# Column quarters for the variances and attn3's row sums, and 1 / sigma through DRAM

## The chip, the cores and the metric

The kernel runs on one core of a Trainium2 chip. A core has five engines that run their own streams of instructions in order and wait for each other on semaphores: TensorE (PE, matmuls; PEld is its weight loads), VectorE (DVE), ScalarE (ACT), GpSimd (POOL) and SyncE (SP, which here issues nearly all DMAs). SBUF holds the working data in 128 partitions, PSUM takes the results of matmuls in banks of 128 x 512 f32, DRAM is the memory off the core. The metric is the device time of one execution in microseconds (us), as a median over runs.

## The reference

Two layers over x, a tensor of 2 images x 512 channels x 2048 positions (tokens) in f32. Layer 0 is softmax attention of 8 heads with 64 channels each. Layer 1 is Nystrom attention with 256 landmarks and a feed-forward step. Each of layer 1's two steps starts with a layer normalization over the 512 channels of a token:

```python
def _ln_t(v, eps=1e-5):
    m = jnp.mean(v, axis=-1, keepdims=True)
    s = jnp.var(v, axis=-1, keepdims=True)
    return (v - m) / jnp.sqrt(s + eps)
...
qL = q.reshape(b, h, m, l, d).sum(axis=3) / l
kL = k.reshape(b, h, m, l, d).sum(axis=3) / l
attn1 = softmax(einsum('bhid,bhjd->bhij', q, kL), axis=-1)
attn2 = softmax(einsum('bhid,bhjd->bhij', qL, kL), axis=-1)
attn3 = softmax(einsum('bhid,bhjd->bhij', qL, k), axis=-1)
attn2_pinv = moore_penrose_iter_pinv(attn2, PINV_ITERS)
out = attn1 @ (attn2_pinv @ (attn3 @ v))
...
t = t + _L1_attn_ref(_ln_t(t), L1_attn_Wqkv, L1_attn_Wout, L1_attn_bout, L1_attn_conv_w)
t = t + _L1_ffn_ref(_ln_t(t), L1_ffn_qidx, L1_ffn_scales, L1_ffn_W)
```

The pseudo-inverse is six iterations of products of 256 x 256 matrices. A convolution of v over 33 tokens is added to layer 1's attention.

## The kernel before

Channels lie in the partitions, tokens along the free dimension. A token block is 512 tokens (TB); an image has four of them. Heads are taken in pairs of 2 x 64 channels, four pairs an image. Everything is f32. The order of instructions on PE, DVE, ACT and POOL is the order in which the program writes them; generators that yield are interleaved by hand to fill one stage's waits with another's work. SP's DMAs are put in order by a scheduler that goes by when they can start. A DMA that waits on SP holds back the ones behind it.

The stages that matter here, in order of time:

- Attention of layer 0 (attention0, up to 1400 us): groups of two steps of scores (L1057), exp on ACT (L1065), a running sum on DVE (L1075) and values (L1087). At the end of a token block the sums over the keys are taken with line 778 (sums_of), inverted (L1102) and spread over the partitions with eight DMAs (L789, spread).
- First normalization, layer 0's output projection with it (norm0_steps over statistics; L956 is the projection yp, L963 adds the residual). For image 0 it is interleaved with attention (787 to 960 us), for image 1 with the projections of layer 1's first pairs (1405 to 1530 us). It calls statistics once a block: adds of channels on DVE (L974, L975), a matmul with a matrix of 1/512 that gives the mean on all partitions (L978), subtraction (L979), squares on ACT (L982, L985), adds (L987, L988), a second matmul for the variance (L991), sqrt on ACT (L993). The reciprocal (L1008) follows one step later, then the products on POOL (L1010) and DVE (L1011) and the store of xh. The squares lie in the buffer of x itself, xb; for image 0 there is one such buffer, and the next block's x is loaded into it (L1021) as soon as the squares are read.
- Layer 1's pairs (1740 to 2600 us): for each of eight pairs the iterations of the inverse (pinv, L1513 to L1536, tiles M and R, product banks pa and pb). Between its steps chunk(c) and last(i) put the next pair's attn3 (L1352, L1366, L1373), the previous pair's attn1 (L1580 to L1617, with sums_of and spread once a block), a convolution (L1450) and the values of the pair after next (L941). At chunk(4) landmarks_values takes attn3's row sums (L1397), inverts them (L1407) and multiplies (L1408, yT); at last(1) it transposes yT (L1416) and loads A for the next pair, which iteration_start turns into M (L1487).
- Finish: output projection of layer 1 (L956), statistics again (the squares are in an own tile sq, the reciprocal is L1641), feed-forward matmuls on the normalized but not yet divided tokens (L1673) and then the product with 1 / sigma (L1662, y), the residual add (L1663) and the store. For image 1 the four blocks lie between the last pairs, for image 0 they are the end of the kernel (from 2660 us). 1 / sigma is thus needed on all 128 partitions for each of 512 tokens.

The matmul with 128 columns of equal weights writes the same sums into all 128 partitions. sums_of instead uses 32 columns per part of the tokens, with the parts beside each other in the array; each part's sums then lie in 32 partitions alone, which is why a spread follows.

Of the kernel before, what the change touches and what calls it, by code (L numbers as in the profile page):

```python
# [10 lines left out]
F32 = mybir.dt.float32  # L11
I32 = mybir.dt.int32
AF = mybir.ActivationFunctionType
ALU = mybir.AluOpType
AX = mybir.AxisListType

P = 128
# [3 lines left out]
HEADS, D = 8, 64  # L21
NPAIR = HEADS // 2
TB = 512
NTB = S // TB
NST = S // P
LM, POOL = 256, S // 256
# [627 lines left out]
Q = P // 4  # L654
# [9 lines left out]
def fast_path(  # L664
# [35 lines left out]
    nc = tc.nc  # L700
    dram = ctx.enter_context(tc.tile_pool(name="dram1", bufs=1, space=bass.MemoryType.DRAM))
# [25 lines left out]
    def chunked(ap):  # L727
        return ap.rearrange("(k p) n -> p k n", p=P)

    def bank(name):  # L730
        return ps.tile([P, 512], F32, tag="pp", name=name)
# [17 lines left out]
    def exps(name):  # L749
        p = ppool.tile([P, 4 * (LM + 1)], F32, tag="p", name=name)  # L750
        return p[:, :1024].rearrange("p (h n) -> p h n", h=2)
# [4 lines left out]
    def row_of(name):  # L756
        return apool.tile([P, TB], F32, tag="rinv", name=name, bufs=3)

    mean_w = const.tile([P, P], F32, name="mean_w1")
    nc.vector.memset(mean_w, 1.0 / C)  # L760
    ones = const.tile([P, D], F32, name="ones1")
    nc.vector.memset(ones, 1.0)
    eps = const.tile([P, 1], F32, name="eps1")
# [5 lines left out]
    csum = const.tile([P, B * NPAIR, 4], F32, name="csum1")  # L769


    def sums_of(rs, acc):


        for h in range(2):
            for j in range(2):
                lo = h * D + j * Q
                nc.tensor.matmul(  # L778
                    rs[lo : lo + Q, :LM], lhsT=ones[:, :Q], rhs=acc[:, h, j * LM : (j + 1) * LM],
                    start=True, stop=True,  # L780
                )

    def spread(dst, few):

        for h in range(2):
            for to in range(2):
                for j in range(2):
                    lo, src = h * D + to * Q, h * D + j * Q
                    nc.sync.dma_start(dst[lo : lo + Q, j * LM : (j + 1) * LM], few[src : src + Q, :])  # L789


    def advance(gens, n=1):
# [13 lines left out]
    def drain(gen):  # L806
        for _ in gen:
            pass
# [159 lines left out]
    def deviation(name):  # L968
        return apool.tile([P, TB], F32, tag="rstd", name=f"rstd_{name}", bufs=1)

    def statistics(xb, xn, part, name, squares, row):


        nc.vector.tensor_tensor(part, xb[:, :2, :], xb[:, 2:, :], ALU.add)  # L974
        nc.vector.tensor_tensor(part[:, 0, :], part[:, 0, :], part[:, 1, :], ALU.add)  # L975
        yield
        mean = bank(f"mean_{name}")
        nc.tensor.matmul(mean, lhsT=mean_w, rhs=part[:, 0, :], start=True, stop=True)  # L978
        nc.vector.tensor_tensor(xn, xb, mean.unsqueeze(1).to_broadcast([P, KC, TB]), ALU.subtract)  # L979
        yield  # L980
        sq, *others = squares()
        nc.scalar.activation(sq, xn[:, :2, :], AF.Square)  # L982
        n = 2 // len(others)
        for i, other in enumerate(others):
            nc.scalar.activation(other, xn[:, 2 + i * n : 2 + (i + 1) * n, :], AF.Square)  # L985
            to = sq[:, i * n : (i + 1) * n, :]
            nc.vector.tensor_tensor(to, to, other, ALU.add)  # L987
        nc.vector.tensor_tensor(sq[:, 0, :], sq[:, 0, :], sq[:, 1, :], ALU.add)  # L988
        yield
        var = bank(f"var_{name}")  # L990
        nc.tensor.matmul(var, lhsT=mean_w, rhs=sq[:, 0, :], start=True, stop=True)  # L991
        rstd = row()
        nc.scalar.activation(rstd, var, AF.Sqrt, bias=eps, scale=1.0)  # L993
        yield rstd

    def out0_units(b, t, xb, oTs):
# [4 lines left out]
    def norm0_steps(b, t, xb, xn, part):  # L1001

        toks = slice(t * TB, (t + 1) * TB)
        name = f"n0_{b}_{t}"
        squares = lambda: (xb[:, :2, :], xb[:, 2:, :])
        for rstd in statistics(xb, xn, part, name, squares, lambda: deviation(name)):
            yield
        nc.vector.reciprocal(rstd, rstd)  # L1008
        wide = rstd.unsqueeze(1).to_broadcast([P, 2, TB])
        nc.gpsimd.tensor_tensor(xn[:, 2:, :], xn[:, 2:, :], wide, ALU.mult)  # L1010
        nc.vector.tensor_tensor(xn[:, :2, :], xn[:, :2, :], wide, ALU.mult)  # L1011
        nc.gpsimd.dma_start(chunked(xh_d[b])[:, :, toks], xn)
        yield
# [185 lines left out]
    class Pair:  # L1199
# [192 lines left out]
        def landmarks_values(self):  # L1392

            rs = bank(f"rs3_{self.name}")
            for j in range(2):
                for h in range(2):
                    nc.tensor.matmul(  # L1397
                        rs[h * D : (h + 1) * D, :LM],
                        lhsT=ones,
                        rhs=self.acc3[:, h, j * LM : (j + 1) * LM],  # L1400
                        start=j == 0,
                        stop=j == 1,
                    )
            rinv = self.acc3[:, 0, :]
            yT = rinv[:, LM:]
            nc.scalar.copy(rinv[:, :LM], rs[:, :LM])
            nc.vector.reciprocal(rinv[:, :LM], rinv[:, :LM])  # L1407
            nc.vector.tensor_tensor(yT, self.av3[:, :LM], rinv[:, :LM], ALU.mult)  # L1408
            X = exps(f"X2_{self.name}").rearrange("p a b -> p (a b)").rearrange("p (h k n) -> p h k n", h=2, k=2)
            self.X = [X[:, h] for h in range(2)]  # L1410
            for h in range(2):
                nc.sync.dma_start(self.X[h], X_d[self.b, self.hp, h])
            yield
            tp = bank(f"tp_{self.name}")
            for t in range(2):
                nc.tensor.transpose(tp[:, t * P : (t + 1) * P], yT[:, t * P : (t + 1) * P], ident)  # L1416
            self.Y = lmpool.tile([P, 2, P], F32, tag="Y", name=f"Y_{self.name}")
            nc.scalar.copy(self.Y, tp[:, :LM].rearrange("p (t n) -> p t n", t=2))
            A = zpool.tile([P, 2, 2, LM + 1], F32, tag="Q", name=f"A_{self.name}")
            self.A = [A[:, h] for h in range(2)]  # L1420
            for h in range(2):
                for t in range(2):
                    cols = slice(t * P, LM)
                    nc.sync.dma_start(self.A[h][:, t, cols], A_d[self.b, self.hp, h][:, t, cols])
            yield
# [193 lines left out]
    class Finish1:  # L1619
# [13 lines left out]
        def steps(self, row):  # L1633
            def squares():
                sq = apool.tile([P, 2, TB], F32, tag="acc", name=f"sq_{self.name}")
                return sq, *(row_of(f"sq{k}_{self.name}").unsqueeze(1) for k in (2, 3))

            self.xn = self.xn()
            for rstd in statistics(self.xb, self.xn, self.xn[:, :2, :], self.name, squares, row):
                if rstd is not None:  # L1640
                    nc.vector.reciprocal(rstd, rstd)  # L1641
                    self.rstd = rstd
                yield

        def norm_units(self):
# [204 lines left out]
    def second_of_first():  # L1850
        pair = todo[0]
        yield from values(0)
        yield from pair.attn3()
        landmarks, start, conv = pair.landmarks_values(), pair.start_values(), convolution(0)
        for part in (landmarks, conv, landmarks, start, conv):
            next(part)
            yield
        drain(conv)
        next(start)
        yield  # L1860
# [26 lines left out]
    for n, pair in enumerate(todo):  # L1887
        before = todo[n - 1] if n else None
        after = todo[n + 1] if n + 1 < len(todo) else None
# [57 lines left out]

        def last(i):
            nonlocal start
            if i == 1 and after:  # L1950
                next(landmarks)
                drain(landmarks)
                start = after.start_values()
            if i == 2 and after:
                next(start)
            else:
                advance(vals)
            if i == 3 and after:
                next(start)
            if n_ones < NTB:  # L1960

                if i == 0:
                    before.attn1_scores(n_ones, 0)
                    before.attn1_scores(n_ones, 1)
                    before.attn1_add(n_ones)
                if i == 1:
                    before.attn1_values(n_ones)
                if i == 2:
                    before.attn1_sums(n_ones)
                if i == 3:  # L1970
                    before.attn1_inverse(n_ones)
                if i == 5:
                    before.attn1_end(n_ones)
            if i == 5:
                pair.attn1_scores(0, 0)
                pair.attn1_scores(0, 1)
            advance(finish)

        landmarks = start = None
# [62 lines left out]
    n = 3 * B * NPAIR  # L2042
# [113 lines left out]
```

## Time and profile before

| | us |
|---|---|
| median of 3 runs (lowest, highest) | 2775.44 (2773.93, 2777.14) |
| the profiled execution, its own time | 2775.64 |
| its span in the profile | 2773.8 |
| variance matmuls L991, busy (16 of them) | 9.3 + 8.6 |
| attn3's row sums L1397, busy (8 of them) | 8.7 |
| reciprocals L1641 and L1008, busy (8 + 8) | 26.8 + 26.7 |
| sqrt L993, busy (16) | 5.5 + 5.5 |
| reciprocal L1407, busy (8) | 14.0 |

A line of the groups names the source line, the engine, the operation, output <- inputs, the tile of the array for matmuls (rows*columns), partitions x elements of the output and the count; after the first bar the busy time in us and the mean of one in ns, after the second the idle time of the engine just ahead of these instructions and what ended it. A line of the timeline gives start and length in us, then the same names; in square brackets the idle time before it and its releaser. Rows of one kind that follow each other are merged, so the gap to the next row's start says more than the length, as the end of a matmul is modelled. SPq is SP issuing DMAs.

### The profile page before, as it was taken

What the parts mean: (1) busy time and instruction counts of PE and PEld (TensorE: products, weight loads), DVE (VectorE), ACT (ScalarE), POOL (GpSimd) and SP (SyncE); (2) the same over time, 40 slices, a digit from 0 to 9 for tenths busy, and PEclk for the clock granted to TensorE, in tenths of its full rate; (3) what the DMA queues carried; (4) which work ended last, traced back from release to release, by engine and by line L of the source; (5) the groups of instructions that cost most, each with busy time, mean ns of one, the idle gap of its engine ahead of it and who ended that gap; (6) DMA issues with size and microseconds to landing.
All of it is one profiled execution on the core that took longest, in us unless ns stands there. A gap on an engine that the chain in (4) does not pass through costs nothing. (4 is left out here: it accounts for less than half of the span.)

```text
span 2773.8 us, 41257 instructions
## 1 busy us (share of the span) xinstructions
PE 2712.4 (98%) x17010; PEld 1365.7 (49%) x17010; DVE 1638.7 (59%) x2076; ACT 905.8 (33%) x1352; POOL 197.2 (7%) x133
## 2 busy tenths in 40 slices
PE   9999999999999999999999999999999999999898
PEld 5343443434343334343344455777677766555334
DVE  3768787774557765747657444544644545556455
ACT  1344343433335244435412223233332323221210
POOL 1101101010001200100002000000000000000000
PEclk9999999999999999999999999999999999999999
DMA  3000000201111200012025532313111202111301
GB/s 115 12 9 9 13 6 7 69 24 50 32 50 54 80 9 7 8 49 64 24 87 186 201 118 92 97 34 115 54 36 58 81 9 90 38 66 31 106 32 47
DMA packets 110358, 157.22 MB, mean 57 GB/s; under 512 B 16065, under 2 KB 67793, under 8 KB 107601
## 3 DMA queue, kind: packets, MB, share of 16 engines
q1 hardware_dynamic: 105664, 137.68, 15.7%
q0 software_dynamic: 4416, 16.79, 1.6%
q8 instruction: 135, 2.21, 0.4%
q14 instruction: 63, 0.51, 0.1%
q10 hardware_dynamic: 80, 0.03, 0.0%
HBM read 82.48 MB, written 55.19 MB: 50 GB/s over the span
## 5 line engine op out<-in xcount | busy, mean ns | idle before, releaser
L1075 DVE TENSOR_TENSOR acc_f<-acc_f,p_f 128x1024 f32<-128x1024 f32 x448 | 589.4, 1316 | 235.6 <-ACT p_f L1065 207.0
L1065 ACT ACTIVATE p_f<-sc_f 128x1024 f32<-128x1024 f32 x512 | 496.4, 1021 | 561.9 <-PE sc_f L1057 550.4
L1057 PE MATMUL sc_f<-q_f,k_f 64*64 64x512 f32 x4096 | 491.7, 595 | 2.4 <-ACT p_f L1065 2.4
L1087 PE MATMUL av_f<-p_f,v_f 64*64 64x512 f32 x4096 | 484.3, 589 | 0.0
L1087 PEld LDWEIGHTS av_f<-p_f,v_f 64*64 64x64 f32 x4096 | 156.5, 133 | 283.0 <-issue 283.0
L1057 PEld LDWEIGHTS sc_f<-q_f,k_f 64*64 64x64 f32 x4096 | 144.8, 133 | 280.9 <-issue 256.0
L1230 PE MATMUL pp<-xh,w 128*128 128x512 f32 x512 | 233.0, 608 | 0.7 <-ACT q L1233 0.7
L1230 PEld LDWEIGHTS pp<-xh,w 128*128 128x128 f32 x512 | 96.5, 194 | 123.2 <-issue 116.0
L1523 PE MATMUL pb<-R 128*128 128x192 f32 (+1 forms) x640 | 151.4, 383 | 1.6 <-DVE M L1536 1.6
L1523 PE MATMUL pa<-M 128*128 128x192 f32 (+1 forms) x640 | 150.6, 380 | 0.0
L941 PEld LDWEIGHTS vp_f<-wv_f,x 128*128 128x128 f32 x1024 | 115.6, 192 | 12.7 <-issue 11.0
L941 PE MATMUL vp<-w,xh 128*128 128x128 f32 x1024 | 120.8, 276 | 0.0
L941 PEld LDWEIGHTS vp<-w,xh 128*128 128x128 f32 x1024 | 117.0, 192 | 7.2 <-issue 4.2
L1523 PEld LDWEIGHTS pb<-R 128*128 128x128 f32 x640 | 107.8, 192 | 25.2 <-DVE M L1536 2.3
L896 PE MATMUL pp_q_f<-x,wq_f 128*128 128x512 f32 x256 | 115.9, 606 | 2.9 <-DMA x<-in_x_dram 1.5
L941 PE MATMUL vp_f<-wv_f,x 128*128 128x128 f32 x1024 | 118.5, 276 | 0.0
L1523 PEld LDWEIGHTS pa<-M 128*128 128x128 f32 x640 | 108.0, 193 | 21.0 <-ACT M L1514 2.5
L956 PE MATMUL yp_g<-o,wo_f 128*128 128x512 f32 x256 | 115.5, 598 | 0.8 <-DVE y_g L1662 0.8
L956 PE MATMUL yp_f<-q_f,wo_f 128*128 128x512 f32 x256 | 114.0, 598 | 2.2 <-issue 1.2
L1673 PE MATMUL fp_g<-xn_g,mT 128*128 128x512 f32 (+1 forms) x264 | 115.7, 589 | 0.0
L896 PE MATMUL pp_k_f<-x,wk_f 128*128 128x512 f32 x256 | 114.1, 599 | 0.4 <-DVE q_f L899 0.4
L1105 POOL TENSOR_TENSOR q_f<-q_f,rinv_f 128x512 f32<-128x512 f32 x32 | 45.9, 1434 | 920.4 <-DMA rinv_f<-acc_f 920.4
(196 smaller groups left out, 2762.0 us busy)
## 6 DMA issues: line engine op xcount, KB each, us to landing
xh<-xh_fd SPq DMA_DIRECT2D x12, 1024.0 KB, 5.4
rinv_f<-acc_f SPq DMA_DIRECT2D x256, 32.0 KB, 1.9
xr_f<-in_x_dram SPq DMA_DIRECT2D x8, 1024.0 KB, 5.2
x_fd<-xr_f POOLq DMA_DIRECT2D x8, 1024.0 KB, 4.6
xh_fd<-xn_f POOLq DMA_DIRECT2D x8, 1024.0 KB, 4.6
k_fd<-k SPq DMA_DIRECT2D x32, 256.0 KB, 2.8
q_fd<-q SPq DMA_DIRECT2D x32, 256.0 KB, 2.9
xb_g<-x_fd SPq DMA_DIRECT2D x32, 256.0 KB, 4.3
```

The source lines that it names most:

```text
L896: nc.tensor.matmul(pp, lhsT=w_sb[kind][:, k, cols], rhs=xbs[t][:, k, :], start=k == 0, stop=k == KC - 1)
L941: nc.tensor.matmul(vp[:, j * P : (j + 1) * P], lhsT=xb[:, k, j * P : (j + 1) * P], rhs=w_of(k), start=k == 0, stop=k == KC - 1,)
L956: nc.tensor.matmul(yp, lhsT=wo_sb[:, k, m * P : (m + 1) * P], rhs=oTs[k][:, toks], start=k == 0, stop=k == NPAIR - 1,)
L1057: nc.tensor.matmul(sc[r * D : (r + 1) * D, h, :], lhsT=hd.k[rows, lo : lo + D], rhs=hd.q[rows, t * TB : (t + 1) * TB], start=True, stop=True,)
L1065: nc.scalar.activation(p, sc, AF.Exp, scale=D**-0.5)
L1075: nc.vector.tensor_tensor(acc, first if c == 1 else acc, p, ALU.add)
L1087: nc.tensor.matmul(av[r][half, :], lhsT=hd.v[keys, c, half], rhs=pp[keys, h, :], start=c == 0, stop=c == NST - 1,)
L1105: nc.gpsimd.tensor_tensor(o, o, rinv, ALU.mult)
L1230: nc.tensor.matmul(pp, lhsT=self.w[j][:, c, :], rhs=xhs[t][:, c, :], start=c == 0, stop=c == KC - 1)
L1523: nc.tensor.matmul(dst, lhsT=lhsT[:, k, t * P : (t + 1) * P], rhs=rhs[:, k, :], start=k == 0, stop=k == 1)
L1673: nc.tensor.matmul(fp[:, cols], lhsT=mT[:, k, m * P : (m + 1) * P], rhs=self.xn[:, k, cols], start=k == 0, stop=k == KC - 1,)
```

## The change

statistics takes the variance with four matmuls of 32 columns each, one per 128 tokens, each into its own 32 partitions. sqrt and reciprocal then work on 128 x 128 elements (few, in the second half of the squares' tile) in place of 128 x 512. One partition of each group of 32 goes to a small DRAM tensor (4 x 128), and a second DMA, which waits for the first, loads it back to all 128 partitions as the 512 values of rstd. The reciprocal now belongs to statistics' last step; in the first normalization it is issued one step earlier than before. attn3's row sums use sums_of with two parts of the free dimension added up (parts=2), eight matmuls of 32 columns x 128 in place of four of 64 x 256; copy and reciprocal work on 128 elements, and the inverse goes through spread (eight DMAs of 16 KB). The product yT is issued one step later: at last(0) in the pairs.

```diff
-    def sums_of(rs, acc):
-        for h in range(2):
-            for j in range(2):
-                lo = h * D + j * Q
-                nc.tensor.matmul(
-                    rs[lo : lo + Q, :LM], lhsT=ones[:, :Q], rhs=acc[:, h, j * LM : (j + 1) * LM],
-                    start=True, stop=True,
-                )
+    def sums_of(rs, acc, parts=1):
+        n = TB // parts // 2
+        for part in range(parts):
+            for h in range(2):
+                for j in range(2):
+                    lo, at = h * D + j * Q, part * 2 * n + j * n
+                    nc.tensor.matmul(
+                        rs[lo : lo + Q, :n], lhsT=ones[:, :Q], rhs=acc[:, h, at : at + n],
+                        start=part == 0, stop=part == parts - 1,
+                    )
 
     def spread(dst, few):
+        n = few.shape[1]
...
-                    nc.sync.dma_start(dst[lo : lo + Q, j * LM : (j + 1) * LM], few[src : src + Q, :])
+                    nc.sync.dma_start(dst[lo : lo + Q, j * n : (j + 1) * n], few[src : src + Q, :])
...
         var = bank(f"var_{name}")
-        nc.tensor.matmul(var, lhsT=mean_w, rhs=sq[:, 0, :], start=True, stop=True)
+        for j in range(4):
+            nc.tensor.matmul(
+                var[j * Q : (j + 1) * Q, :P], lhsT=mean_w[:, :Q], rhs=sq[:, 0, j * P : (j + 1) * P],
+                start=True, stop=True,
+            )
+        few = sq[:, 1, :P]
+        nc.scalar.activation(few, var[:, :P], AF.Sqrt, bias=eps, scale=1.0)
+        nc.vector.reciprocal(few, few)
+        rstd_d = dram.tile([4, P], F32, name=f"rstd_d_{name}")
+        nc.sync.dma_start(rstd_d, few[::Q, :])
         rstd = row()
-        nc.scalar.activation(rstd, var, AF.Sqrt, bias=eps, scale=1.0)
+        nc.sync.dma_start(rstd, rstd_d.rearrange("j n -> (j n)").partition_broadcast(P))
         yield rstd
...
-        nc.vector.reciprocal(rstd, rstd)
         wide = rstd.unsqueeze(1).to_broadcast([P, 2, TB])
...
             rs = bank(f"rs3_{self.name}")
-            for j in range(2):
-                for h in range(2):
-                    nc.tensor.matmul(
-                        rs[h * D : (h + 1) * D, :LM],
-                        lhsT=ones,
-                        rhs=self.acc3[:, h, j * LM : (j + 1) * LM],
-                        start=j == 0,
-                        stop=j == 1,
-                    )
-            rinv = self.acc3[:, 0, :]
-            yT = rinv[:, LM:]
-            nc.scalar.copy(rinv[:, :LM], rs[:, :LM])
-            nc.vector.reciprocal(rinv[:, :LM], rinv[:, :LM])
-            nc.vector.tensor_tensor(yT, self.av3[:, :LM], rinv[:, :LM], ALU.mult)
+            sums_of(rs, self.acc3, 2)
+            few, rinv, yT = self.acc3[:, 0, :P], self.acc3[:, 0, LM:], self.acc3[:, 1, :LM]
+            nc.scalar.copy(few, rs[:, :P])
+            nc.vector.reciprocal(few, few)
+            spread(rinv, few)
...
+            yield
+            nc.vector.tensor_tensor(yT, self.av3[:, :LM], rinv, ALU.mult)
             yield
...
             for rstd in statistics(self.xb, self.xn, self.xn[:, :2, :], self.name, squares, row):
-                if rstd is not None:
-                    nc.vector.reciprocal(rstd, rstd)
-                    self.rstd = rstd
+                self.rstd = rstd
                 yield
...
-        for part in (landmarks, conv, landmarks, start, conv):
+        for part in (landmarks, conv, landmarks, landmarks, start, conv):
             next(part)
             yield
...
         def last(i):
             nonlocal start
+            if i == 0 and after:
+                next(landmarks)
             if i == 1 and after:
                 next(landmarks)
                 drain(landmarks)
```

## The prediction

> **What bounds the kernel now.** I read the page first: where the busy time lies.
>
> ```profile
> PE 2712.4 (98%) x17010; PEld 1365.7 (49%) x17010; DVE 1638.7 (59%) x2076; ACT 905.8 (33%) x1352; POOL 197.2 (7%) x133
> ```
>
> TensorE (PE) is busy for 98% of the span. Time taken off PE is worth its full length, but only where nothing else then ends later: each of the touched places must be read alone. Second, the groups by line and shape (busy us and mean ns of one stand behind the bar):
>
> ```profile
> L1641 DVE RECIPROCAL rstd_g<-rstd_g 128x512 f32<-128x512 f32 x8 | 26.8, 3350 | 15.9 <-ACT rstd_g L993 15.9
> ...
> L778 PE MATMUL rs_f<-acc_f,ones 128*32 128x256 f32 x256 | 20.4, 391 | 3.9 <-DVE acc_f L1075 3.7
> ...
> L991 PE MATMUL var_g<-sq_g,mean_w 128*128 128x512 f32 x16 | 9.3, 666 | 0.3 <-DVE sq_g L988 0.3
> ...
> L1397 PE MATMUL rs<-acc,ones 128*64 128x256 f32 x64 | 8.7, 392 | 0.0
> ```
>
> A matmul in f32 is two records: 16 variances are 32 of L991. Line 778 is the model of what is new: four 128*32 matmuls at once. Third, the timeline of PE, for what such a group costs from start to start:
>
> ```profile
> 2663.26 0.64 PE L778 MATMUL rs<-acc,ones 128*32 128x256 f32 x8
> 2663.83 7.13 PE L956 MATMUL yp_g<-o,wo_f 128*128 128x512 f32 x16
> ...
> 2693.39 1.02 PE L991 MATMUL var_g<-sq_g,mean_w 128*128 128x512 f32 x2
> 2694.24 13.90 PE L956 MATMUL yp_g<-o,wo_f 128*128 128x512 f32 x32
> ```
>
> A variance takes 0.85 there. Fourth, the timeline of VectorE (DVE) where 1 / sigma is made and used: the last one of the first normalization (L1011 multiplies by it), then one in the finish.
>
> ```profile
> 943.70 3.35 DVE L1008 RECIPROCAL rstd_n<-rstd_n 128x512 f32<-128x512 f32 x1
> 947.08 1.23 DVE L1011 TENSOR_TENSOR xn_f<-xn_f,rstd_n 128x1024 f32<-128x1024 f32 x1
> 948.23 1.75 DVE L1102 RECIPROCAL acc_f<-rs_f 128x256 f32<-128x256 f32 x1
> ```
>
> ```profile
> 2474.04 0.68 DVE L1662 TENSOR_TENSOR y_g<-fp_g,rstd_g 128x512 f32<-128x512 f32 x1
> 2474.76 1.26 DVE L1663 TENSOR_TENSOR xb_g<-y_g,xb_g 128x512 f32<-128x512 f32 x1
> 2475.94 0.54 DVE L1487 TENSOR_SCALAR M<-A,zs 128x256 f32<-128x256 f32 x2
> ```
>
> Last the DMA issues (KB each, median us to landing), and SyncE's (SP) queue just before that second place:
>
> ```profile
> rinv<-acc SPq DMA_DIRECT2D x256, 32.0 KB, 1.8
> ...
> w<-in_wqkv_dram SPq DMA_DIRECT2D x24, 256.0 KB, 3.4
> ...
> o_fd<-o SPq DMA_DIRECT2D x8, 256.0 KB, 2.3
> ...
> A_fd<-A SPq DMA_DIRECT2D x16, 64.0 KB, 2.0
> ```
>
> ```profile
> 2466.92 4.94 SPq L789 DMA_DIRECT2D rinv<-acc  x8
> ```
>
> Eight spread DMAs hold SP for 4.94 us.
>
> **What the Trainium skill says.** "TensorEngine Tiling (Array Packing)", Key Properties: tiles run their loads and matmuls in parallel, and a change of tiling mode drains the array. The trace agrees: eight records of 391 ns in line 778 end within 0.57 (2663.26 to 2663.83), and they start 0.2 after the eight yp before them, at 0.43 each (13.74 / 32), are due. "DMA: Bandwidth & Descriptors", Anatomy of one DMA (written for GpSimd's queue): about 2.0 us fixed for any transfer, most of it the receipt of the last byte; the trace has 1.8 to 2.0 for 32 to 64 KB. "Perfetto Trace Analysis", Tensor Engine Instruction: DVE and ScalarE (ACT) run strictly in order; so a DVE instruction that waits for a DMA holds all behind it, as the trace shows (908.16: 5.89 idle for xr_f).
>
> **The change, part by part.** A quarter has 128 columns in place of the 256 of line 778: 2 x 0.107 less than 0.57, so 0.36, plus the drain of 0.2. Against 0.85 between 128*128 neighbours this saves 0.3; between 64*64 neighbours the variance costs 1.16 now (0.1 before it, 1.06 to the next start, at 790.3), and saves 0.65. attn3's sums cost 0.92 (2203.50 to 2204.42) and become 0.57 and a drain: 0.3 saved. In total 10 x 0.3 + 4 x 0.4 + 2 x 0.65 + 8 x 0.3 = 8.3 us at most.
>
> The reciprocal falls from 3.35 to 0.95 (line through 1.75 at 256 and 3.35 at 512), sqrt from 0.69 to about 0.3. Added is a round trip that the trace does not show as such: a 2 KB store, 2.0 (A_fd), and a 256 KB load that SP may issue only when the store has landed, 2.8 (between o_fd's 2.3 and w's 3.4). What stands ahead of what on each queue I took from the order of the changed kernel's instructions. With handovers 5.0; bounds 4.3 and 7, as loads that stood in line took 4.3 to 5 (xb_g, L). So 1 / sigma is ready at 0.3 + 0.95 + 5.0 = 6.25 after its input, against 4.05: 2.2 later, while DVE has 2.4 less work.
>
> First normalization, image 0 (var at 790, 853, 902, 938). The next x load goes into the buffer that now holds the few values, so it waits for the store, and stands behind the rstd load on SP. First: x lands at 801, used at 806; saved 0.7. Second: sqrt ends 855.5, store lands 858.6, x issued at 859 lands 864.2; the residual add frees the bank for rs at 865.0 against 865.09: 0. Third: x lands at 912.5, not 908; the third yp waits for the first's bank until 913.3 in place of 909.6; 2.8 of idle PE at mean_n (925.23) take back part: +1.5 late. Fourth: no work stands between reciprocal (943.70, ends 944.65) and L1011: DVE waits until 949.6 where it went on at 947.08; behind it stand the sums' reciprocal and the adds that free ACT's buffers (ACT waits 2.74 there already), and PE follows ACT: +2.2. Sum +3.0.
>
> Image 1 (1440, 1462, 1488, 1512). The short reciprocal now stands ahead of the next block's adds, which mean_n waits for: +1.0 (behind a table load), -0.4, +0.65, -0.3. L1011's load has landed in time in all four. Sum +0.95.
>
> Finish of image 1 (2337, 2465, 2549, 2610). First and third: over 7 us of other work stand between reciprocal and use: -0.4, -0.3. Second: the store is issued behind the eight spreads, at 2471.9; the load lands at 2476.75; y starts 2.75 late, then its add (without GpSimd's contention), then M: p_pa at 2479.0 in place of 2477.27: +1.7. Fourth: the same 2.5 late behind spreads, but the bank is due only at 2622.9: -0.3. Sum +0.7.
>
> Last block (2671, 2693, 2723, 2752): PE idles 4.95 for GpSimd after the first: 0; the others have 14 us of matmuls ahead of the use: -0.9.
>
> attn3's sums: copy, reciprocal, then eight spread DMAs: few is ready 2.5 after the sums start, the last DMA is issued 4.35 later and lands after 2.2, so yT is there at 9.5; the transposes are due at 11.1. Convolution and the values' matmuls cover it: 5 x -0.3. Where a store goes ahead on SP (todo 6) +0.2, todo 7: 0. In the very first the reciprocal comes late (1711); yT is ready at 1718.8 but its transposes are due at 1717: +1.4. Sum +0.1.
>
> Total: 3.0 + 0.95 + 0.7 - 0.9 + 0.1 = +3.85. The profiled execution took 2775.64 (span 2773.8 and 1.8 around it), 0.2 over the median 2775.44; so 2779.5 profiled, 2779.3 as median.
>
> **The rivals.** (a) Not covered: store and load take 7 rather than 5. Four places pay the whole (fourth of image 0; second and fourth of the finish; the first attn3 in its landing), two the store's half: 4 x 2 + 2 x 1 = 10 less 1 of slack, +13: 2788. It decides from 0.5 us more on the round trip, since three and a half payers carry +3.85 past +5.5. For it: loads that took 4.3 to 5; against it: rinv's 1.8. (b) All covered: 8.3 saved less the half that mean_n and GpSimd hold back anyway at least 1.5: -7, 2768. For it: DVE loses 16 x 2.4 = 38 us of work; against it: the two DVE places above, with nothing between. (c) The quarters don't run side by side: each variance then costs 1.06 in place of 0.86 (the drain on top), attn3's sums 1.9 in place of 0.92: 16 x 0.2 + 8 x 1 = 11 more, and the savings of about 4.8 counted above are gone: +20, 2795. Against it: line 778.
>
> **How the numbers follow.** Forecast 0.60 (own range 2774 to 2784; of it 0.23 over the bound), (a) 0.20, (b) 0.14, (c) 0.06. A measurement of this kernel can tell about 0.2%, 5.5 us, from no change. Slower: 0.23 + 0.20 + 0.05 = 0.48; faster: 0.11 of (b); same: 0.41. The range 2771 to 2789 takes in (a) and leaves out most of (b) and (c).
>
> **What would show it.** Right: L991 near 0.4 from start to start; PE idle at L956 near 913, at p_pa near 2479 with DVE waiting for rstd; L1011 waiting for a DMA near 945. Wrong: rstd loads landing within 2 us, or DVE waits for the spread in each pair.

## The result

The changed kernel takes 2787.86 us (five runs, 2786.43 to 2789.82) beside 2773.93 us for the kernel before on the same chip (five runs, 2773.41 to 2777.14). The ratio is 1.0049, 95% interval 1.0038 to 1.0061: slower by 13.9 us. The profiled execution took 2786.43 us with a span of 2784.7. The busy times of the changed kernel's page:

```profile
PE 2708.1 (97%) x17170; PEld 1363.0 (49%) x17170; DVE 1590.5 (57%) x2076; ACT 899.9 (32%) x1352; POOL 191.1 (7%) x133
```

TensorE has 4.3 us less to do (2712.4 before) and VectorE 48 less, and the span is 10.9 us longer. What was to become shorter did, as the groups by line and shape show (busy us, mean ns of one, then idle time ahead):

```profile
L1024 DVE TENSOR_TENSOR xn_f<-xn_f,rstd_n 128x1024 f32<-128x1024 f32 x8 | 9.7, 1217 | 9.9 <-DMA rstd_n<-rstd_d_n 9.9
...
L1003 DVE RECIPROCAL xr_f<-xr_f 128x128 f32<-128x128 f32 x8 | 7.6, 950 | 2.4 <-ACT xr_f L1002 2.4
...
L781 PE MATMUL rs<-acc,ones 128*32 128x128 f32 x128 | 5.2, 279 | 0.0
...
L997 PE MATMUL var_n<-xr_f,mean_w 128*32 128x128 f32 x64 | 3.4, 285 | 1.7 <-DVE xr_f L992 1.6
```

Line 997 is the variance (L991 before), 781 with 128x128 attn3's sums, 1003 the reciprocal, 1024 the product with 1 / sigma (L1011). The first of these lines is the new cost: 9.9 us in which VectorE waited for the load of 1 / sigma. One timeline gives the largest loss, TensorE in the third block of image 0:

```profile
901.14 0.43 PE L997 MATMUL var_n<-xr_f,mean_w 128*32 128x128 f32 x8 [1.64 <-DVE xr_f L992]
901.50 7.13 PE L960 MATMUL yp_f<-q_f,wo_f 128*128 128x512 f32 x16
913.60 9.78 PE L960 MATMUL yp_f<-q_f,wo_f 128*128 128x512 f32 x16 [4.97 <-DVE xr_f L967]
923.31 0.46 PE L884 MATMUL fp_q_f<-emb_f,weq_f 64*128 64x96 f32 x2
```

The variance takes 0.36 from start to start. Then sixteen yp (records; a matmul has two) go by at the usual pace, TensorE stands 4.97 us, and the next sixteen take 9.71 us (913.60 to 923.31), where sixteen take 6.97 elsewhere in the same trace (1460.30 to 1467.27). The releaser in the brackets is VectorE's residual add; its own timeline and SP's say what that waited for:

```profile
912.79 0.75 DVE L967 SCALAR_TENSOR_TENSOR xr_f<-yp_f,b_f,xr_f 128x512 f32<-128x512 f32 x1 [8.98 <-DMA xr_f<-in_x_dram]
...
903.84 0.53 SPq L1005 DMA_DIRECT2D rstd_d_n<-xr_f  x1
905.50 0.33 SPq L1007 DMA_DIRECT2D rstd_n<-rstd_d_n  x1
906.00 0.39 SPq L1034 DMA_DIRECT2D xr_f<-in_x_dram  x1
```

The next block's x (L1034) goes out behind the trip (the store of the few values of 1 / sigma to DRAM and the load back), at 906.00, and lands 6.8 us later. The fourth block stops in another way, on VectorE first, then on ScalarE, then on TensorE:

```profile
946.36 0.95 DVE L1003 RECIPROCAL xr_f<-xr_f 128x128 f32<-128x128 f32 x1
953.50 1.23 DVE L1024 TENSOR_TENSOR xn_f<-xn_f,rstd_n 128x1024 f32<-128x1024 f32 x1 [6.20 <-DMA rstd_n<-rstd_d_n]
...
958.10 1.94 ACT L1078 ACTIVATE p_f<-sc_f 128x1024 f32<-128x1024 f32 x2 [6.88 <-DVE acc_f L1088]
...
959.18 3.02 PE L1070 MATMUL sc_f<-q_f,k_f 64*64 64x512 f32 x16 [3.95 <-ACT p_f L1078]
961.96 2.58 PE L1100 MATMUL av_f<-p_f,v_f 64*64 64x512 f32 x16
```

VectorE stands 6.20 us for 1 / sigma, the adds behind it are late, ACT finds no free buffer until an add has run (L1088), and TensorE waits for ACT. Both stops have a slow stretch after them, and so has the stop in the finish that is shown below. Windows cut where TensorE's granted clock changes show it (window, length, PE busy, clock, DMA share, GB/s):

```profile
908.71:912.12 3.41, 0.00 (x0) 1.00 0.77 290
912.12:918.95 6.83, 5.35 (x7) 0.50 0.35 134
956.50:959.91 3.41, 0.73 (x8) 1.00 0.46 161
959.91:963.32 3.41, 3.41 (x20) 0.50 0.68 219
2485.67:2489.08 3.41, 1.43 (x5) 1.00 0.09 29
2489.08:2492.49 3.41, 3.41 (x10) 0.50 0.19 67
```

The clock is halved for 3.41 us, or for twice that, each time after 3.41 us in which TensorE was busy for 0 to 1.43 us. The three halvings start a whole number of such stretches apart: 47.79 us from the first to the second is 14 times 3.4133, and 1529.17 us from the second to the third is 448 times that. So the clock changes on a fixed grid in this trace, and a stop can fall into one stretch of the grid or across two. How little work in a stretch it takes isn't shown: 1.63 us (2615.38 to 2618.79) left the clock at 1.00 here, but in the trace of the kernel before it was halved once after 2.67 us of work (1431.32 to 1434.73).

In the first normalization of image 1 it is x again, twice (VectorE, then SP):

```profile
1459.49 0.75 DVE L967 SCALAR_TENSOR_TENSOR xr_f<-yp_f,b_f,xr_f 128x512 f32<-128x512 f32 x1 [4.39 <-DMA xr_f<-in_x_dram]
...
1482.51 0.75 DVE L967 SCALAR_TENSOR_TENSOR xr_f<-yp_f,b_f,xr_f 128x512 f32<-128x512 f32 x1 [3.89 <-DMA xr_f<-in_x_dram]
...
1452.38 0.39 SPq L1790 DMA_DIRECT2D xr_f<-in_x_dram  x1
```

TensorE stands 0.65 and 0.94 us before a yp for these. The second block of the finish of image 1 is the last place, in SP's, VectorE's and TensorE's timelines:

```profile
2476.68 4.95 SPq L793 DMA_DIRECT2D rinv<-acc  x8
2481.74 0.53 SPq L1005 DMA_DIRECT2D rstd_d_g<-sq_g  x1
2483.34 0.33 SPq L1007 DMA_DIRECT2D rstd_g<-rstd_d_g  x1
...
2486.68 0.69 DVE L1666 TENSOR_TENSOR y_g<-fp_g,rstd_g 128x512 f32<-128x512 f32 x1 [2.75 <-DMA rstd_g<-rstd_d_g]
...
2488.51 0.30 PE L1519 MATMUL p_pa<-ident,M 128*128 128x128 f32 x1 [1.98 <-DVE M L1493]
2488.81 3.55 PE L1529 MATMUL pa<-M 128*128 128x192 f32 x8
2492.15 0.42 PE L1519 MATMUL p_pa<-ident,M 128*128 128x128 f32 x1
```

The store goes out behind eight spreads, y waits 2.75 us, TensorE 1.98, and p_pa with its eight pa takes 3.64 us (2488.51 to 2492.15) where it took 1.84 before (2477.27 to 2479.11).

### The profile page after: what moved, and what is told of

It is laid out like the page before. It is cut to its first block, busy times and chain, and to the rows that moved or that the text cites. A ratio compares the mean times of both kernels' runs of the same rounds, so it can differ in the third digit from the quotient of the medians.

```text
span 2784.7 us, 41782 instructions
## 1 busy us (share of the span) xinstructions
PE 2708.1 (97%) x17170; PEld 1363.0 (49%) x17170; DVE 1590.5 (57%) x2076; ACT 899.9 (32%) x1352; POOL 191.1 (7%) x133
## 5 line engine op out<-in xcount | busy, mean ns | idle before, releaser
L1088 DVE TENSOR_TENSOR acc_f<-acc_f,p_f 128x1024 f32<-128x1024 f32 x448 | 589.1, 1315 | 236.1 <-ACT p_f L1078 206.8
```

The lines of the kernel that those rows point to most:

```text
L1088: nc.vector.tensor_tensor(acc, first if c == 1 else acc, p, ALU.add)
```

## The experiments

The change, eleven variants of it, and a kernel of loads alone, which is not in the table. Measured times are medians; the ratio is to the kernel before on the same chip.

| kernel | us | ratio to before, 95% interval |
|---|---|---|
| the change | 2787.86 | 1.0049 (1.0038 to 1.0061) |
| variances only | 2787.98 | 1.0058 (1.0044 to 1.0071) |
| attn3 only | 2778.45 | 1.0014 (1.0007 to 1.0021) |
| image 0 as before | 2780.45 | 1.0024 (1.0016 to 1.0032) |
| covered places only | 2776.82 | 1.0009 (1.0000 to 1.0017) |
| own row, GpSimd's queue (image 0) | 2783.53 | 1.0033 (1.0020 to 1.0045) |
| stops filled with matmuls | 2794.96 | 1.0070 (1.0056 to 1.0084) |
| and the fourth product on GpSimd | 2777.47 | 1.0011 (1.0003 to 1.0020) |
| second place of the finish by GpSimd's queue | 2785.90 | 1.0039 (1.0026 to 1.0053) |
| very first attn3 as before | 2782.64 | 1.0036 (1.0022 to 1.0050) |
| all mended | 2776.96 | 1.0011 (1.0003 to 1.0020) |
| five variances only | 2773.26 | 0.9997 (0.9988 to 1.0005) |

The theory after the result: the trip is paid where VectorE or the x load stands behind it, and each stop of TensorE is paid a second time by a slow stretch. Rivals: the extra spreads on SP, a loss spread evenly, traffic of the memory.

**Which half of the change.** Variances alone: landmarks_values, last and second_of_first as before.

```diff
-            sums_of(rs, self.acc3, 2)
+            for j in range(2):
+                for h in range(2):
+                    nc.tensor.matmul(rs[h * D : (h + 1) * D, :LM], lhsT=ones,
+                        rhs=self.acc3[:, h, j * LM : (j + 1) * LM], start=j == 0, stop=j == 1)
...
-            if i == 0 and after:
-                next(landmarks)
```

> All 16 variances with quarters, attn3's row sums as before the change. Theory (the variances' trip through DRAM is paid in the first normalization, attn3 about cancels itself: +1.9 in the very first, 5 x -0.3 to -0.4, +0.3): about 11 us over the kernel before, 2783 to 2787. Rival (attn3's 64 extra spread DMAs on SP are what delays the others): within 5 us of the kernel before, under 2779.

And attn3 alone, with the variance of the kernel before:

```diff
-        for j in range(4):
-            nc.tensor.matmul(
-                var[j * Q : (j + 1) * Q, :P], lhsT=mean_w[:, :Q], rhs=sq[:, 0, j * P : (j + 1) * P],
...
+        nc.tensor.matmul(var, lhsT=mean_w, rhs=sq[:, 0, :], start=True, stop=True)
+        rstd = row()
+        nc.scalar.activation(rstd, var, AF.Sqrt, bias=eps, scale=1.0)
```

> attn3's row sums with quarters, all variances and full-width reciprocals as before the change. Theory: within 1.5 us of the kernel before, 2772.5 to 2775.5, because what the very first one loses the others give back. Rival (attn3's spreads cost): 2779 or more.

The variances bring 12.9 us (2787.98 beside 2775.04; by the ratio 16), a little over the theory's range. attn3 alone brings 3.4, between the two expectations: it doesn't cancel itself. By its trace, against the kernel before, the very first costs 2.3 (shift -0.83 to +1.46), five pairs give 1.65 back, and there is one loss that the theory had not, 1.8 us: in the fourth block of the finish attn1's spreads land late, and TensorE stands 2.35 us for them, where it stood 0.55 before. This isn't tied to attn3, though: the same stop is 1.72 us in the trace of the variances alone, which has none of attn3's spreads, and 0.70 in that of the changed kernel, which has them all. VectorE, then TensorE, of the attn3-only kernel:

```profile
2602.03 0.69 DVE L1630 TENSOR_TENSOR rinv<-av,rinv 128x512 f32<-128x512 f32 x1 [4.33 <-DMA xb_g<-x_fd]
...
2602.78 1.94 PE L1610 MATMUL av<-p,u 128*64 128x512 f32 x8 [2.35 <-DVE rinv L1630]
```

These two kernels serve as references for the changed one: starts of the same TensorE instruction, set side by side, show where it falls behind. Above the line against attn3 alone (so the effect of the variances), below it against the variances alone (the effect of attn3):

```
                                        reference   changed    shift
before the first variance                  773.01    771.53    -1.48
first variance passed                      792.36    790.19    -2.17
sums after the second block's stop         866.12    864.51    -1.61
embedding after the third block's yp       918.67    923.31    +4.64
projection after the third mean_n          927.98    930.54    +2.56
embedding after the fourth stop            957.02    964.47    +7.45
last mean_n of image 1                    1491.51   1502.06   +10.55
tp of the pair before finish, place 2     2458.23   2467.49    +9.26
second p_pa after finish, place 2         2479.35   2492.15   +12.80
scores after finish, place 4              2612.78   2623.43   +10.65
last block, place 4                       2755.00   2764.49    +9.49
----
before the very first attn3 sums          1517.04   1516.55    -0.49
values after them                         1750.66   1752.07    +1.41
convolution six pairs later               2324.91   2324.45    -0.46
```

Image 0 holds +8.9 of it (-1.48 to +7.45), image 1 +3.1, the finish +1.1 (9.59, the shift at its start at 2321, to 10.65), the last block -1.2; the very first attn3 +1.9, the next six pairs together -1.9. Such sums from single traces are good to 1 to 2 us, since each trace, the reference too, has late spreads and stretches of half clock of its own. For the finish this matters: the reference has the stop of 2.35 us there; against the kernel before itself the finish costs 2.1 (the shift goes from 10.00, at 2331.15, to 12.07, at 2625.43).

**Image 0 alone.** The old variance and the old place of the reciprocal for the four blocks of image 0:

```diff
-        for j in range(4):
+        if not name.startswith("n0_0"):
+            for j in range(4):
...
+        else:
+            nc.tensor.matmul(var, lhsT=mean_w, rhs=sq[:, 0, :], start=True, stop=True)
```

> The changed kernel, but with the four variances of the first normalization of image 0 as before the change. Theory: this one stretch of four places holds +8.5 of the +14 us, so about 2779 (2777.5 to 2781). Rival (a lower TensorE clock or a loss spread evenly over all places): at most a quarter of it goes, 2784 or more.

2780.45: 7.4 us less than the changed kernel (6.9 by the ratios), in the theory's range; an even loss is out.

**Only where it looked covered.**

```diff
-        for j in range(4):
+        if name in ("g_1_0", "g_1_2", "g_0_1", "g_0_2", "g_0_3"):
+            for j in range(4):
...
-        landmarks, start, conv = pair.landmarks_values(), pair.start_values(), convolution(0)
+        landmarks, start, conv = pair.landmarks_values_whole(), pair.start_values(), convolution(0)
```

> Quarters only where the trace shows the trip covered: variances 1 and 3 of the finish of image 1, 2 to 4 of the last block, attn3's sums in all pairs but the very first; all else as before the change. Theory: 2 x -0.4, 3 x -0.3, 5 x -0.35 and +0.3 for one pair: -3.1, so 2770 to 2772, 0.1% faster than the kernel before. Rival (every trip on SP has its price wherever it stands): 2775 or more.

A miss: 2776.82 over 13 runs, 1.8 over the kernel before, where the theory had 3 under it. The profiled run was the fastest of the 13 (2773.53) and does show the gain: from 1506 to 2338 the instructions come 2.2 us earlier step by step. It too has the stop of 2.31 us at the fourth block of the finish. To tell whether attn3's spreads or each trip take the rest, the same without attn3 (the old landmarks_values for all pairs):

> The covered-only kernel without its part of attn3: the kernel before with quarters in five variances alone, 1 and 3 of the finish of image 1 and 2 to 4 of the last block. Theory (attn3's spreads ate what the covered-only kernel should have gained: a late landing of spreads shows in its trace and in that of attn3 alone): 2 x -0.4 and 3 x -0.3, 1.7 us under the kernel before, 2771 to 2774 beside a kernel before of 2774 to 2775. Rival (each trip costs something, also these five): 1 us or more over the kernel before.

2773.26 beside 2774.24: the theory's range, with an interval that holds no change at all. So the trips of these five cost nothing that can be told apart, and what the covered-only kernel lacks points to its part of attn3; the two intervals overlap.

**x behind the trip.** In image 0 the few values go into the tile of 1 / sigma itself, not into x's buffer, and the trip goes by GpSimd's queue:

```diff
-        few = sq[:, 1, :P]
+        early = name.startswith("n0_0")
+        rstd = row() if early else None
+        few = rstd[:, :P] if early else sq[:, 1, :P]
+        queue = nc.gpsimd if early else nc.sync
...
-        nc.sync.dma_start(rstd_d, few[::Q, :])
-        rstd = row()
+        queue.dma_start(rstd_d, few[::Q, :])
+        rstd = rstd if early else row()
```

> The changed kernel, but in image 0's first normalization the few values lie in the tile of 1 / sigma itself and not in the x buffer, and store and load go on GpSimd's queue, so that the next x load waits for neither. Theory (in the third place PE stood because x was issued late, behind the trip): TensorE's idle before the third yp goes from 4.97 us to under 2 and the slow stretch behind it with it; the fourth place stays, DVE waits for 1 / sigma there as before. 2781 to 2784. Rival (the third place is late through 1 / sigma itself, or through traffic): the idle stays over 4, 2787 or more.

2783.53, as the theory said. TensorE and SP of this kernel:

```profile
905.36 10.57 PE L960 MATMUL yp_f<-q_f,wo_f 128*128 128x512 f32 x24
916.64 3.70 PE L960 MATMUL yp_f<-q_f,wo_f 128*128 128x512 f32 x8 [0.71 <-DVE xr_f L967]
...
905.53 0.37 SPq L1037 DMA_DIRECT2D xr_f<-in_x_dram  x1
```

x now goes out right behind the variance (0.5 us after its start, not 4.9), 24 yp run through at full pace, and the stop of 4.97 is 0.71. In the fourth block, with no x load beside the trip, VectorE still waited 5.75 us. The edit changes the buffer and the queue at once; which of the two held x back was not tested apart.

**VectorE behind the trip.** On top of that, both halves of the fourth product on GpSimd:

```diff
-        nc.vector.tensor_tensor(xn[:, :2, :], xn[:, :2, :], wide, ALU.mult)
+        eng = nc.gpsimd if name == "n0_0_3" else nc.vector
+        eng.tensor_tensor(xn[:, :2, :], xn[:, :2, :], wide, ALU.mult)
```

> The experiment with the own row and GpSimd's queue, and in the fourth place of image 0 both halves of the multiplication by 1 / sigma on GpSimd, so that VectorE doesn't wait for the trip there. Theory (VectorE's 5.75 us wait in front of the scores' row sums is what stops TensorE for 3.45 us, with a slow 1.5 behind it): the stop falls under 1 us, and the time by 4 to 5 from 2783.5, to 2778.5 to 2780. Rival (ACT is late for its own sake, or GpSimd's second half holds something else): 2782 or more.

2777.47, better than expected. VectorE goes from the reciprocal straight on to the sums, and TensorE has no stop at the place of the 3.95 us:

```profile
944.05 0.95 DVE L1006 RECIPROCAL rstd_n<-rstd_n 128x128 f32<-128x128 f32 x1
944.92 1.70 DVE L1119 RECIPROCAL acc_f<-rs_f 128x256 f32<-128x256 f32 x1
...
952.79 1.90 PE L1074 MATMUL sc_f<-q_f,k_f 64*64 64x512 f32 x16
954.51 1.90 PE L1104 MATMUL av_f<-p_f,v_f 64*64 64x512 f32 x16
```

With two edits 10.4 us of the 13.9 are gone: what stands behind the trip, x's load and VectorE's work, is shown as the cause in image 0. Against the kernel before, image 0 costs 8.5 us in the changed kernel's trace (the shift goes from -0.44 to +8.04), and in this one it gains 2.4 (+2.28 to -0.09).

**The slow stretch.** More matmuls into unused columns of the variance's bank, so that TensorE doesn't stand:

```diff
+        for _ in range({"n0_0_2": 6, "n0_0_3": 5}.get(name, 0)):
+            nc.tensor.matmul(var[:, P:], lhsT=mean_w, rhs=sq[:, 0, P:], start=True, stop=True)
```

> The changed kernel with 6 and 5 more matmuls of 384 columns (0.65 us each, 3.9 and 3.2 us) into unused columns of the variance's bank, behind the third and the fourth variance of image 0: their results go nowhere. They take place in time in which TensorE stood idle later on. Theory (a stop of 4 to 5 us brings a lower clock, which cost 2.8 us in the third place and some 1.6 in the fourth): the stops shrink to 1 us or so, the sixteen yp behind the third take about 7 us in place of 9.7, and the time falls to 2783 to 2785 although 7 us of work were added. Rival (the clock falls whatever TensorE does, or the stop alone is the loss): 2787 to 2795.

As a time it is a miss, 2794.96; the trace says why, and it answers for one place. VectorE and TensorE of this kernel:

```profile
909.70 0.95 DVE L1005 RECIPROCAL xr_f<-xr_f 128x128 f32<-128x128 f32 x1 [4.38 <-ACT xr_f L1004]
...
920.81 8.55 PE L960 MATMUL yp_f<-q_f,wo_f 128*128 128x512 f32 x16 [4.68 <-DVE xr_f L967]
...
965.04 2.00 PE L1072 MATMUL sc_f<-q_f,k_f 64*64 64x512 f32 x16 [0.90 <-ACT p_f L1080]
966.87 1.90 PE L1102 MATMUL av_f<-p_f,v_f 64*64 64x512 f32 x16
```

In the third block sqrt waited for the added matmuls too, since they write the same bank: the reciprocal starts 4.9 us after the variance in place of 1.7, the trip and x are as much later, and the stop stays at 4.68. There the edit tests nothing. In the fourth the reductions ahead of the reciprocal cover that; the stop is 0.90, and scores and values take 3.66 us (965.04 to 968.70) in place of 5.29 (959.18 to 964.47). Between the fourth variance and that point the kernel gains 2.1 us on the changed one although 3.4 us of matmuls were added: here the slow stretch came with the stop. Over all of image 0 it loses 0.7; the other 6 us of the time lie elsewhere, in the profiled run 3.6 at the very start and single late landings later on. They are not explained.

**The trip itself.** A kernel of loads alone:

```diff
+            nc.sync.dma_start(row, rows[:, n, :TB])
...
+            nc.sync.dma_start(row, x[0][n, :TB].partition_broadcast(P))
...
+            nc.sync.dma_start(row[:, :P], x[0][n, :P].partition_broadcast(P))
```

> Everything but a copy of x to the output is left out; ahead of it loads of one tile of 128x512 one after the other, three of each kind: the store and load of the trip; 128 different rows of 2 KB; one row of 2 KB to all 128 partitions; the same in two halves on two queues; a quarter of it (128x128); and one row while a 1 MB load is under way on another queue. Theory (traffic beside it made the load long): one row alone takes 2.5 to 3.2 us from issue to use, as 128 rows do, and 4.4 or more beside the 1 MB load. Rival (128 reads of the same 2 KB are slow in themselves): one row alone takes 4.4 to 4.9, 128 rows 2.5 to 3.2, the quarter about a quarter of the difference over 2 us.

The copies of x to the output didn't stay behind the loads: they ran beside all kinds but the last two, and the 1 MB load meant for the last kind ran at the start. So the last two kinds are those without traffic, a quarter of a row and one row (issue, then VectorE's look at it):

```profile
75.11 6.84 SPq L40 DMA_DIRECT2D row<-in_x_dram  x3
78.37 0.15 DVE L23 COPY seen<-row 128x1 f32<-128x1 f32 x1 [3.29 <-DMA row<-in_x_dram]
81.44 0.15 DVE L23 COPY seen<-row 128x1 f32<-128x1 f32 x1 [2.91 <-DMA row<-in_x_dram]
...
84.72 6.89 SPq L45 DMA_DIRECT2D row<-in_x_dram  x3
87.81 0.15 DVE L23 COPY seen<-row 128x1 f32<-128x1 f32 x1 [3.11 <-DMA row<-in_x_dram]
91.10 0.15 DVE L23 COPY seen<-row 128x1 f32<-128x1 f32 x1 [3.14 <-DMA row<-in_x_dram]
```

One row to all partitions takes 3.1 us, a quarter of it 2.9 to 3.3. Beside 1 MB copies 128 different rows took 3.7 to 5.4 and one row 3.8 to 5.3. So reading one row 128 times isn't slow in itself, and traffic is; in the changed kernel x's 1 MB goes out 0.5 us behind the load, which then takes 4.4 to 4.9 (949.07 to 953.50; 793.67 to 798.56). In the kernel with the own row, on GpSimd's queue and with no x beside it, the fourth block's load takes 3.5 (947.74 to 951.20). Between 64 and 256 KB the size hardly counts. 128 different rows were not measured without traffic. The Trainium skill, "DMA: Bandwidth & Descriptors", Anatomy of one DMA, which is written for GpSimd's queue, gives a fixed cost of about 2.0 us for any transfer; by these runs most of the time is fixed too, but about 3 us lie between issue and use on SP.

**The second place of the finish.**

```diff
-        nc.sync.dma_start(rstd_d, few[::Q, :])
+        queue = nc.gpsimd if name in ("g_1_1",) else nc.sync
+        queue.dma_start(rstd_d, few[::Q, :])
```

> The changed kernel, with store and load of the second place of the finish of image 1 alone on GpSimd's queue, ahead of which nothing stands, in place of SP's, where eight spreads go first. Theory: the load is issued about 5 us earlier, y isn't held, p_pa's 1.98 us stop and the slow matmuls behind it go (3.3 us), of which the stop before the fourth place's row sums takes back 1.6: 1.5 to 3.5 us under the changed kernel, 2784.5 to 2786.5. Rival (y waits for the trip itself): 2787 or more, the stop stays.

The time, 2785.90, fits the theory, though its interval holds no difference from the changed kernel; the trace contradicts it. VectorE, GpSimd and TensorE:

```profile
2487.49 0.69 DVE L1623 TENSOR_TENSOR rinv<-av,rinv 128x512 f32<-128x512 f32 x1 [5.39 <-DMA rinv<-acc]
...
2481.88 0.60 POOL L1008 DMA_DIRECT2D rstd_g<-rstd_d_g  x1 [1.36 <-DMA rstd_d_g<-sq_g]
...
2490.49 0.45 PE L1520 MATMUL p_pa<-ident,M 128*128 128x128 f32 x1 [2.41 <-DVE M L1494]
```

y waits no more, but the product ahead of it does: the eight spreads, issued until 2483.18, are there at 2487.49, 4.3 us after the last issue, where in the changed kernel it was 1.6 (2481.63 to 2483.24). The load of 1 / sigma now runs in their midst. "DMA: Bandwidth & Descriptors", Issuing engines are not separate DMA queues, says that the transfers of all issuing engines run on the same 16 DMA engines and interleave; this one trace agrees. The wait has moved to another instruction.

**The very first attn3, and all mended.** The old row sums for the first pair alone, then that with the own row and GpSimd's queue for both images and for places 2 and 4 of the finish, and the fourth product on GpSimd:

```diff
-        landmarks, start, conv = pair.landmarks_values(), pair.start_values(), convolution(0)
+        landmarks, start, conv = pair.landmarks_values_whole(), pair.start_values(), convolution(0)
...
-        early = name.startswith("n0_0")
+        early = name.startswith("n0") or name in ("g_1_1", "g_1_3")
```

> The changed kernel, with attn3's row sums of the very first pair alone as before the change. Theory (its transposes stand 2.1 us for the spread): 1.5 to 2.5 us under the changed kernel, 2785.5 to 2786.5. Rival (the convolution that follows takes the stop back): 2787.5 or more.

> All mendings together: own row and GpSimd's queue in both images' first normalization and in places 2 and 4 of the finish, the fourth multiplication of image 0 on GpSimd, attn3's very first row sums as before the change. Theory: 2783.5 less 4.5 (fourth place), 2 (image 1), 2 (finish), 1.9 (very first attn3) = 2773, 2771 to 2775: at best 0.1% under the kernel before. Rival (each trip keeps some of its price wherever it stands, as the covered-only run suggests): 2776 or more.

The first gains 5.2 us, more than expected (by the ratios 3.6, with intervals that overlap): 1.8 at the sums themselves by the trace (the shift goes from -0.76 to -2.60) and 1.7 in the second place of the finish, where nothing was edited. TensorE of this kernel there:

```profile
2486.42 0.30 PE L1554 MATMUL p_pa<-ident,M 128*128 128x128 f32 x1 [1.81 <-DVE M L1528]
2486.73 1.99 PE L1564 MATMUL pa<-M 128*128 128x192 f32 x8
2488.56 0.27 PE L1554 MATMUL p_pa<-ident,M 128*128 128x128 f32 x1
```

It still stands 1.81 us, but p_pa with its eight pa takes 2.14 us, not 3.64: the stop lies across two stretches of the clock's grid, with 3.08 and 1.94 us of work in them (2481.53 to 2484.94 to 2488.36), and the clock stays at 1.00. So nearly the same stop brings the slow stretch in one trace and not in another.

All mended is 2776.96, the rival's value: its 13 runs go from 2773.04 to 2783.18, those of the kernel before from 2771.80 to 2777.97. In its trace TensorE still stands 1.99 us before p_pa.

## Why the prediction came out as it did

The forecast of 2779.3 gave the sign and the places, and was 8.6 us short: +3.85 in the sum, 13.9 measured. Its range held the time only because it was drawn to take in rival (a); the forecast's own range, 2774 to 2784, did not. By its steps:

- Variance and sums: right. A variance goes from start to start in 0.36; it saves 0.7 in the first two places of image 0 and about 0.3 in the last block; six of attn3's pairs give 1.9 together. Rival (c), no concurrency, is out.
- "First: ... saved 0.7", "Second: ... 0": the first is right; in the second x landed at 863.7, 0.5 before the time in the text, but the sums still stood 1.2 us for the adds behind it: +0.6.
- "Third: x lands at 912.5 ... third yp waits ... until 913.3": it landed at 912.79, and yp went on at 913.60. But "+1.5 late" became +4.2 (-1.61 to +2.56): the step counted the stop alone. The sixteen yp after it took 9.71 us in place of 6.97, 2.7 more.
- "Fourth: ... +2.2": +4.9 (2.56 to 7.45). Trip 6.2 in place of 5.0, and 1.75 of slow stretch: scores, values and all until the embedding took 5.29 us, and 3.54 (952.79 to 956.33) without the stop.
- Image 1, +0.95: measured +3.1. The first block's adds behind the reciprocal cost 0.86 as said; left out was x behind the trip, which stopped yp for 0.65 and 0.94, although the same queue had been counted in image 0.
- Finish: the second place was right in mechanism and stop (y 2.75 late, as in the text), but p_pa and pa after it cost 1.8 more. A part came back by the fourth place: +1.1 against the attn3-only kernel, +2.1 against the kernel before, in place of +0.7.
- Last block -0.9: -1.2. The very first attn3 +1.4: +1.9. Whether "todo 7: 0" holds isn't shown: late spreads stop TensorE in that stretch in some traces, with attn3's quarters and without.

The term that was too small is thus the price of a stop, which the text counted at its length alone. The three slow stretches cost 2.7 + 1.75 + 1.8 = 6.3 us, x in image 1 1.6, the longer trip 1.2 in the fourth block: 9.1 of the 10.05 us by which the sum fell short, though what later stops gave back isn't subtracted. "TensorE: Matmul & The Clock Gate", Part 1, says that TensorE goes to half its clock after an idle window of about 3.4 us and needs about as long a busy one to come back, and that the window runs free of the kernel. The trace agrees in the rate (0.50 from 2489.08 to 2492.49, 1.00 ahead of it), in the length of 3.41 us and in the grid. It differs in what counts as idle: TensorE stood only 1.98 us, and was busy for 1.43 of the 3.41 us ahead of the drop.

Rival (a) named 2788 and gave half the reason: the trip is 6.2 to 6.5 us where a load of x goes out behind it (947.33 to 953.50 from the store's issue; 792.03 to 798.56), not 7, and at the three and a half payers of the text the 1.2 us more would have brought some 4 us. That its 2788 met the time is luck: the slow stretches made up the rest. Rival (b), all covered, fell on both VectorE places.

Open: why attn1's spreads land late at the fourth place of the finish in some traces (2.35 us of stop in the attn3-only kernel, 2.31 in the covered-only one, 1.72 with the variances alone, but 0.70 in the changed kernel and 0.55 before); and why the covered-only kernel and the mended one have medians 2 to 3 us above what their traces add up to. Stops for late spreads show up singly (1.82 us at tp in the kernel with filled stops), and a stop may or may not bring half clock. That the two make up the rest is argued, not shown; the variances-only kernel, without attn3's spreads, varies by 7.9 us over five runs, the covered-only one, with them, by 7.3 over 13.

## What to carry to other kernels

A small result that goes through DRAM (2 KB out, 256 KB back) took 5.5 to 6.5 us here from the store's issue to its use, and the engine that waits in order for it, and the loads queued behind it on SP, pay that, not the one that made it: place it where all of these have other work, or put the waiting instruction on an idle engine and keep the trip out of the load's queue and buffer. Don't price a stop of TensorE of 2 to 5 us at its length alone: three here cost 1.75 to 2.7 us more, for 3.41 or 6.83 us of half clock behind them, and a fourth, of 1.81 us in another trace, cost its length and 0.3. Which it is depends on where the clock's grid falls, so plan for the dearer case. Saving 0.3 us of matmul eight or sixteen times isn't worth a wait of that kind: even the version with only five covered trips (ratio 0.9997, 0.9988 to 1.0005) can't be told from the kernel before.

## What the hardware showed unexpectedly

A stop of 1.98 us was enough for half the clock over 3.41 us (p_pa and pa at 3.64 in place of 1.84 us), while one of 1.81 us at the same place, in the kernel with the very first attn3 as before, lay otherwise on the clock's grid and was not. A 64 KB load took 2.9 to 3.3 us and a 256 KB one of the same kind 3.1. And moving a DMA to another queue (the finish's trip to GpSimd's) held back transfers already issued on SP: eight 32 KB spreads landed 4.3 us after their last issue, not 1.6.
